# Coefficient-network loads and first-projection stores moved from SyncE to GpSimd in a four-layer vision kernel

## The chip, the cores and the metric

The kernel runs on one core of one Trainium2 chip. The metric is the device time of one execution in microseconds (us). Before the change it is 5452.3 us, the median of three runs (5446.23 to 5452.5). The kernel works in float32 throughout.

The engines are named as the profile names them: PE (TensorE), DVE (VectorE), ACT (ScalarE), POOL (GpSimd) and SP (SyncE). SP computes nothing here: it only begins DMAs. POOL and ACT can begin DMAs as well, each in the order of its own instruction stream.

## The reference

A batch of 8 images of 56 x 56 positions and 192 channels passes four residual layers, each `x = x + layer(groupnorm(x))`. Layers 0 and 1 are Toeplitz layers, layer 2 is a 7 x 7 depthwise convolution with an MLP, layer 3 is window attention. The change concerns layers 0 and 1, which compute:

```python
p = silu(x @ p_w.T + p_b); q = silu(x @ q_w.T + q_b); v = silu(x @ v_w.T + v_b)   # 192 -> 576
a1 = rpe_mlp(positions, t1_...) * decay     # positions -55..55; 4 small layers 1->32->32->32->32->576
a2 = rpe_mlp(positions, t2_...) * decay     # decay = (0.95 + 0.05*clip(slope, 0, 1)) ** |distance|
qv = q * v
o1 = toeplitz(qv along w, a1); o2 = toeplitz(qv along h, a2)
out = (p * (o1 + o2)) @ o_w.T + o_b
```

So each of the two layers needs two tables of coefficients (111 distances by 576 channels), and each table comes out of a small network of width 32 (the coefficient network) and a decay per channel. The tables don't depend on x.

## The kernel before

**Work on x.** Images go in pairs of pairs: `j0` is 0 or 2, and stands for four images. `tno_qv` (L224) is the first projection: it loads x in groups of 256 positions (L240, tile name `t6`, three buffers), normalizes on ACT (L246), multiplies with the q and v weights on PE (L263, or L284 for the first two groups), adds the bias on DVE (L272, tile `t8`, three buffers), applies silu on ACT (L301), multiplies q by v on POOL (L304, tile `t4`, three buffers) and stores the product in DRAM (L307). The stores are held back by one unit: `multiply` begins with the store of the unit before. One unit is 128 positions by up to 512 of the 1152 columns; a full unit's store is 128 partitions of eight rows of 512 bytes, 512 KB.

`tno_toeplitz` (L365) reads that product back (L380, L383), reads 32 x 60 blocks of the table (L393), and multiplies on PE (L406). ACT copies the result out (L413), DVE turns it (L424, L426), POOL adds the second direction (L429) and stores the sum (L436). `tno_out` (L484) does the rest of the layer.

**Tables.** `decay_tables` (L136) is a generator that makes the two tables of one layer. It loads the slopes 128 channels at a time into a tile of two buffers (L145), raises them to powers on DVE (L146 to L158), then for each of two networks loads its small arrays with six DMAs (L165 to L174, two buffers of each, shared by both layers), runs the three hidden layers (PE L180, DVE L182), and for each 128 channels the last layer (PE L187), clears a tile's end on POOL (L191), multiplies with the decay on DVE (L194) and stores the result in DRAM as a table (L204: four DMAs of 512 rows of 240 bytes per 128 channels).

**Order.** `tno_layers` (L681) writes the order of the first part out by hand. First come the statistics of x (L210, L217), then the first projection of layer 0 for `j0` = 0 in two generators: `first` (columns 0 to 511, all positions) and `rest` (columns 512 to 1151). The loop at L730 takes, for each of 28 turns, a piece of the statistics of the other images, a unit of `first` or `rest`, and a step of each layer's `decay_tables`. On PE, DVE, ACT and POOL the instructions stand in exactly this order. SP's stream is made from the same program: a DMA of SP stands where the program begins it, so a DMA that must wait holds up all that stand behind it. In the built program each DMA of SP also waits until the DMA eight places before it on SP has landed, as they share eight semaphores in turn; the DMAs of POOL have eight of their own.

After that come five lanes, made by `weave` (L644). A lane is a list of generators run one after the other with the pieces of one `tno_toeplitz` woven in at a rate given by estimated times. The Toeplitz generator's first piece only begins its first loads and is counted at 8.0 (L451); the computing pieces count 3.2 each. The pieces are given out when the lane's work has passed the share `lo` (0.04 if not set) and are all out at `hi` (0.92). Lane 0 holds what is left of `rest` and then the projection of the other four images; lanes 1 to 3 hold the rest of layers 0 and 1. The SBUF of the table stage (pool `tab`) is given up before lane 0, and the Toeplitz tiles (pool `tz`) take its place, so in the built program the first loads of lane 0 wait for the last table stores of both layers.

Of the kernel before, what the change touches and what calls it, by code (L numbers as in the profile page):

```python
# [12 lines left out]
F32 = mybir.dt.float32  # L13
# [18 lines left out]
D1 = 576  # L32
# [11 lines left out]
class Net:  # L44
# [91 lines left out]
    def decay_tables(self, L, p, tables):  # L136

        nc, inp = self.nc, self.inp
        tv = p.tile([32, 111], F32, name=f"{L}tv", bufs=1)
        nc.sync.dma_start(tv, inp["tvec"])  # L140
        pows = []
        for c in range(5):
            m = min(128, D1 - 128 * c)
            sl = p.tile([128, 1], F32, name=f"{L}sl")
            nc.sync.dma_start(sl[:m], inp[f"{L}_slope"][128 * c : 128 * c + m, :])  # L145
            nc.vector.tensor_scalar(sl[:m], sl[:m], 0.0, 1.0, ALU.max, ALU.min)  # L146
            nc.vector.tensor_scalar(sl[:m], sl[:m], 1.0 - 0.95, 0.95, ALU.mult, ALU.add)
            pw = p.tile([128, 64], F32, name=f"{L}pw", bufs=5)
            nc.gpsimd.memset(pw[:m, 0:1], 1.0)
            n = 1  # L150
            while n < 64:
                nc.vector.tensor_scalar(
                    pw[:m, n : 2 * n], pw[:m, 0:n], sl[:m], None, ALU.mult
                )
                n *= 2
                if n < 64:
                    sq = p.tile([128, 1], F32, name=f"{L}sl")
                    nc.vector.tensor_mul(sq[:m], sl[:m], sl[:m])  # L158
                    sl = sq
            pows.append(pw)  # L160
            yield 1.0
        for d in range(2):
            t = f"{L}_t{d + 1}"
            w0 = p.tile([32, 2], F32, name="w0")
            nc.sync.dma_start(w0[:, 0:1], inp[f"{t}_w0"])  # L165
            nc.sync.dma_start(w0[:, 1:2], inp[f"{t}_b0"])
            ws = p.tile([32, 3, 32], F32, name="ws")
            nc.sync.dma_start(ws, inp[f"{t}_ws"])
            bs = p.tile([32, 3], F32, name="bs")
            nc.sync.dma_start(bs, inp[f"{t}_bs"])  # L170
            wo = p.tile([32, D1], F32, name="wo")
            nc.sync.dma_start(wo, inp[f"{t}_wo"])
            bo = p.tile([128, 5], F32, name="bo")
            nc.sync.dma_start(bo, inp[f"{t}_bo"])  # L174
            h = p.tile([32, 111], F32, name=f"{L}h")
            nc.vector.tensor_scalar(h, tv, w0[:, 0:1], w0[:, 1:2], ALU.mult, ALU.add)
            nc.vector.tensor_scalar(h, h, 0.0, None, ALU.max)
            for i in range(3):
                hp = self.bank2()[:32, 0, :111]
                nc.tensor.matmul(hp, ws[:, i, :], h, start=True, stop=True)  # L180
                h = p.tile([32, 111], F32, name=f"{L}h")
                nc.vector.tensor_scalar(h, hp, bs[:, i : i + 1], 0.0, ALU.add, ALU.max)  # L182
                yield 1.0
            for c in range(5):
                m = min(128, D1 - 128 * c)
                ap = self.bank2()[:, 0, :111]
                nc.tensor.matmul(  # L187
                    ap[:m], wo[:, 128 * c : 128 * c + m], h, start=True, stop=True
                )
# [31 lines left out]
        for more in self.all_norms():  # L221
            pass

    def tno_qv(self, L, j0, xs, gn, qv, apart=None, cols=(0, 2 * D1), g0=0):  # L224

        nc, p, inp = self.nc, self.tp, self.inp
# [68 lines left out]
        def multiply(m, n, z, at, c0):  # L297
            k = n // 128
            for f in stores:
                f()  # L300
            nc.scalar.activation(z[:m, :n, :], z[:m, :n, :], AF.Silu)  # L301
            prod = p.tile([128, 4, DC * 4], F32, name="t4")
            half = z[:m, :n, :].rearrange("p (n h c) b -> p n h (c b)", h=2, c=DC)
            nc.gpsimd.tensor_mul(prod[:m, :k], half[:, :, 0], half[:, :, 1])  # L304
            n0 = c0 // 128
            stores[:] = [
                lambda: nc.sync.dma_start(  # L307
                    qv[2 * n0 : 2 * n0 + 2 * k, at : at + m, :].rearrange("n t e -> t n e"),
                    prod[:m, :k].rearrange("p n (h e) -> p (n h) e", h=2),
                )  # L310
            ]
# [53 lines left out]
    def tno_toeplitz(self, j0, mats, qv, o):  # L365
# [82 lines left out]
        for n in range(2):  # L448
            loaded.append(load(n))
            matrices(n)  # L450
        yield 8.0  # L451

        work = []

# [226 lines left out]
    def tno_layers(self, x0, x1, x2, gn, last):  # L681
# [18 lines left out]
        with ExitStack() as ctx, ExitStack() as wqp:  # L700
# [2 lines left out]
            Q = lambda i, j0, *more: self.tno_qv(LS[i], j0, x[i], gn[i], qvs[j0], *more)  # L703
            O = lambda i, j0, woven=True: self.tno_out(LS[i], j0, x[i], gn[i], o[i], x[i + 1], gn[i + 1], woven)
            TZ = lambda i, j0: self.tno_toeplitz(j0, tables[i], qvs[j0], o[i])
            QT, OT, TZT = 25 * 2.25 * 5.3, 28 * 10.7, 8 + 72 * 3.2

            with tc.tile_pool(name="tab", bufs=2) as tab:
                stats = [self.input_stats(x0, gn[0], j, tab) for j in range(4)]
                for more in stats[0]:  # L710
                    pass
                first, rest = Q(0, 0, tab, (0, 512)), Q(0, 0, None, (512, 2 * D1), 2)
                next(first)

# [12 lines left out]
                decay = [self.decay_tables(LS[i], tab, tables[i]) for i in range(2)]  # L727
                more = (dt for st in stats[2:] for dt in st)
                with tc.manual_schedule(engines=ENGINES):
                    for n in range(28):  # L730
                        next(more, None)
                        if n == 18:
                            next(rest)
                        if next(first, None) is None:
                            next(rest)
                        if n < 21:
                            next(decay[0])
                        if n >= 7:
                            next(decay[1])
                        if n in (14, 21):  # L740
                            qv = qvs[0 if n == 14 else 2]
                            to = qv[:, T:].rearrange("n (p k) e -> p n (k e)", p=112)
                            nc.gpsimd.dma_start(to, view(none, 0, [[0, D1 // 32], [1, 512]]))
                    for more in decay:
                        assert next(more, None) is None
                lanes = [[(rest, QT * 5 / 9 * 21 / 25 - 25.0), (Q(0, 2), QT)], [(O(0, 0), OT), (Q(1, 0), QT)]]
                parts = [Q(1, 2, None, cols) for cols in ((0, 512), (512, 2 * D1))]
                lanes += [[(O(0, 2), OT), (parts[0], QT * 4 / 9)], [(parts[1], QT * 5 / 9), (O(1, 0), OT)]]
                lanes += [[(O(1, 2, False), OT)]]
            in_order = tc.manual_schedule(engines=ENGINES)  # L750
            with tc.tile_pool(name="tz", bufs=1) as self.tz, in_order:
# [1 line left out]
                for i in range(2):  # L753
                    self.tms.append(self.tz.tile([128, 32 * self.TW], F32, name=f"tm{i}"))
                for n, tz in enumerate((TZ(0, 0), TZ(0, 2), TZ(1, 0), TZ(1, 2))):
                    self.weave(lanes[n], tz, lanes[n + 1][0][0], TZT)
                wqp.close()
            self.weave(lanes[4], **last())

# [915 lines left out]
```

## Time and profile before

| | |
|---|---|
| median of three runs | 5452.3 us |
| the profiled execution's own time | 5448.52 us |
| its span, first to last instruction | 5446.5 us |
| busy: PE, DVE, ACT, POOL | 5166.3, 2588.6, 2384.0, 1767.5 us |
| mean granted PE clock | 0.978 |
| DMA moved | 1116.48 MB, 205 GB/s on average |
| first matmul of the projection | at 27.82 us |
| first Toeplitz matmul | at 378.06 us |

A profile page gives busy times by engine, the span in 40 slices, DMA queues (q1 is the hardware queue of SP, q10 that of ACT, q0 the software queue of POOL), groups of instructions by line, and DMA issues. "Idle before, releaser" says what ended the idle time of an engine ahead of an instruction. A waits view sums those by the instruction that waited: total us, times, longest. A windows view gives the busy time of each engine in a stretch. Lines are L numbers of the kernel before.

### The profile page before, as it was taken

Reading aid. Unit: us, or ns where it says so; the run is one execution under the profiler, and the core shown is the slowest. Engines: PE = TensorE matmul, PEld = TensorE weight load, DVE = VectorE, ACT = ScalarE, POOL = GpSimd, SP = SyncE. Lnnn points to the kernel's source line nnn. Section 1 sums busy time; section 2 is a strip of 40 time slices with the busy share of each in tenths; the row PEclk is TensorE's granted clock in tenths of the full one; section 3 lists DMA queues with packets and bytes.
Section 4 is the critical chain, followed back from the end, with each engine's and each line's share of the span. In section 5 each row is a group of like instructions: output and inputs, shape, how many; then the busy total and the mean of one; then the engine's idle time right before and its main releaser. Section 6 shows DMA issues by size and latency. Waiting matters only on the chain.

```text
span 5446.5 us, 144346 instructions
## 1 busy us (share of the span) xinstructions
PE 5166.3 (95%) x64672; PEld 3811.3 (70%) x64672; DVE 2588.6 (48%) x3990; ACT 2384.0 (44%) x3179; POOL 1767.5 (32%) x1291
## 2 busy tenths in 40 slices
PE   7879999999999999999999899989999999999998
PEld 4657777777777777777777778855665444777776
DVE  6535556455555555645566322422212331566665
ACT  3345555444554454655454322242323333444443
POOL 2225675233664333645443100000001100333333
PEclk9889999999999999999999999999999999999999
DMA  7699997887786999888897666634444221445442
GB/s 253 149 242 280 289 315 228 274 279 256 248 267 170 327 309 308 277 233 280 296 325 246 205 219 237 221 127 161 140 165 121 74 69 49 84 97 108 99 103 68
DMA packets 1051146, 1116.48 MB, mean 205 GB/s; under 512 B 235200, under 2 KB 986304, under 8 KB 1036128
## 3 DMA queue, kind: packets, MB, share of 16 engines
q1 hardware_dynamic: 911584, 854.88, 52.7%
q0 software_dynamic: 38144, 200.99, 9.6%
q10 hardware_dynamic: 100800, 51.38, 3.7%
q8 instruction: 508, 8.32, 0.6%
q14 instruction: 110, 0.90, 0.1%
HBM read 743.17 MB, written 363.94 MB: 203 GB/s over the span
## 4 chain that ended last, share of the span: by engine, by line
PE 49%; DMA 3%; DVE 2%; issue 1%; ACT 1%; POOL 1%; SPq 1%; ACTq 0%; POOLq 0%; DVEq 0%
PE bank L976 7%; PE bank L837 5%; PE bank L1056 5%; PE bank L1250 4%; PE bank L263 3%; PE bank L592 3%; PE bank L1070 3%; PE bank L536 3%; PE bank L1366 2%; PE bank L1280 2%; PE bank L1197 2%; PE bank L1321 2%; PE bank L586 1%; PE bank L406 1%; PE bank L1340 1%
## 5 line engine op out<-in xcount | busy, mean ns | idle before, releaser
L263 PE MATMUL bank<-wq,t 128*128 128x256 f32 (+4 forms) x7680 | 1289.1, 374 | 73.5 <-DVE t L272 43.7
L263 PEld LDWEIGHTS bank<-wq,t 128*128 128x128 f32 (+2 forms) x7680 | 1004.9, 190 | 351.6 <-issue 92.5
L272 DVE TENSOR_TENSOR t<-bank,wq 128x1024 f32<-128x1024 f32 (+3 forms) x480 | 517.7, 1112 | 691.4 <-PE bank L263 540.9
L304 POOL TENSOR_TENSOR t<-t 128x1024 f32<-128x1024 f32 (+2 forms) x288 | 528.4, 1848 | 673.9 <-ACT t L301 338.5
L413 ACT COPY ot<-bank 128x896 f32<-128x896 f32 x576 | 493.2, 909 | 511.5 <-PE bank L406 401.8
L429 POOL TENSOR_TENSOR s<-s,ot 128x1568 f32<-128x1568 f32 x128 | 550.9, 4305 | 197.4 <-DVE ot L426 137.7
L301 ACT ACTIVATE t<-t 128x2048 f32<-128x2048 f32 (+2 forms) x288 | 423.2, 1488 | 330.5 <-DVE t L272 320.5
L406 PE MATMUL bank<-q,tm 56*32 56x224 f32 x18432 | 505.1, 354 | 18.7 <-DMA tm<-L_tab 11.6
L406 PEld LDWEIGHTS bank<-q,tm 56*32 56x32 f32 x18432 | 340.2, 106 | 145.3 <-issue 84.1
L122 POOL DMA_DIRECT2D x<-t x112 | 87.0, 777 | 1087.6 <-DVE t L601 1022.9
L555 ACT ACTIVATE bank<-bank,wo 128x448 f32<-128x448 f32 x448 | 262.9, 606 | 386.2 <-PE bank L545 361.2
L560 DVE TENSOR_TENSOR t<-t,bank 128x896 f32<-128x896 f32 x224 | 242.7, 1087 | 397.8 <-ACT bank L555 339.8
L976 PE MATMUL bank<-z,w 128*128 128x448 f32 (+1 forms) x1344 | 414.4, 556 | 1.5 <-ACT h L985 1.5
L536 PE MATMUL bank<-t,wo 128*128 128x224 f32 x1792 | 372.0, 361 | 21.4 <-ACT t L515 10.2
L536 PEld LDWEIGHTS bank<-t,wo 128*128 128x128 f32 x1792 | 334.9, 192 | 51.0 <-issue 30.2
L592 PE MATMUL bank<-t,wo 128*128 128x224 f32 x1792 | 368.9, 359 | 0.0
L592 PEld LDWEIGHTS bank<-t,wo 128*128 128x128 f32 x1792 | 329.9, 190 | 31.2 <-issue 31.2
L837 PEld LDWEIGHTS bank<-xt,cm 113*112 113x112 f32 x3072 | 316.1, 180 | 42.8 <-issue 33.9
L837 PE MATMUL bank<-xt,cm 113*112 113x108 f32 (+2 forms) x3072 | 324.4, 265 | 10.8 <-ACT h L985 5.7
L976 PEld LDWEIGHTS bank<-z,w 128*128 128x128 f32 (+1 forms) x1344 | 183.0, 189 | 206.7 <-issue 198.7
L127 POOL DMA_DIRECT2D x<-x x64 | 36.7, 574 | 843.4 <-DVE x L1007 813.5
L424 DVE STREAM_TRANSPOSE s<-ot 128x1792 f32<-128x1792 f32 x144 | 292.8, 2034 | 23.0 <-ACT ot L413 14.8
(162 smaller groups left out, 6972.8 us busy)
## 6 DMA issues: line engine op xcount, KB each, us to landing
q<-qv SPq DMA_DIRECT2D x36, 3584.0 KB
t<-L_sum SPq DMA_DIRECT2D x112, 1008.0 KB
L_sum<-s POOLq DMA_DIRECT2D x256, 392.0 KB, 7.3
qv<-t SPq DMA_DIRECT2D x192, 512.0 KB
cm<-in_L_cm SPq DMA_DIRECT2D x96, 896.0 KB
tm<-L_tab SPq DMA_DIRECT2D x288, 240.0 KB
q<-qv SPq DMA_DIRECT2D x40, 1568.0 KB
q<-qv ACTq DMA_DIRECT2D x32, 1568.0 KB
```

Source lines behind the costliest of these rows:

```text
L263: nc.tensor.matmul(pp[:m, b, 256 * j : 256 * j + k], x[rows, j, 2 if part else b, s : s + m], w[rows, part, c0 + c : c0 + c + k],  start=p ...
L272: nc.vector.tensor_add(z[:m, c : c + k, :], view(pp[:m], 0, [[1, k], [256, 4]]), view(bias[:m], c0 + c, [[1, k], [0, 4]]),)
L301: nc.scalar.activation(z[:m, :n, :], z[:m, :n, :], AF.Silu)
L304: nc.gpsimd.tensor_mul(prod[:m, :k], half[:, :, 0], half[:, :, 1])
L406: nc.tensor.matmul(pt[32 * j : 32 * j + 32, r, hf * 224 : (hf + 1) * 224], tm[rows, at : at + 32], q[rows, :, 4 * c : 4 * c + 4], start=Tr ...
L413: nc.scalar.copy(view(ot, 4 * (g % 4), [[16, 2], [32, 112], [1, 4]]), view(pt, 0, [[512, 2], [4, 112], [1, 4]]),)
L424: nc.vector.transpose(to, of.rearrange("p (i k) -> p i k", k=32))
L429: add.tensor_add(to, to, view(of, 0, [[1, 28], [32, 56]]))
L536: mm(gs[c // 2][:, b, c % 2 * 256 : c % 2 * 256 + N], pw[:, 0, 128 * c : 128 * c + 128], xn[:, b], start=c % 2 == 0, stop=False,)
L592: mm(P[:, b, :N], ow[:, c, 0:128], g[:, 4 * b + c], start=False, stop=c == 3)
L837: nc.tensor.matmul(pc[:, 128 * e + 4 * m0 : 128 * e + 4 * m1], cm[:113, e, k, :], xt[:, m0 - 1 + k : m1 - 1 + k, c + e, :], start=n == 0 a ...
L976: nc.tensor.matmul(phs[c][:, s, :TT], w0[rows, part, at : at + 128], z[rows, Z[2 if part else s], :], start=part == flip, stop=part != flip,)
```

## The change

The 36 small loads of the two layers' coefficient networks, slopes and positions become 32 DMAs of POOL that stand ahead of all projection work. The slopes of a layer come in two DMAs into one tile. The arrays of the four networks (two layers, two networks) share tiles of 128 partitions, each network on its own 32, so that none waits for another to give up a buffer; `h` and the PSUM results of the hidden layers lie on the same partitions. `tvec` is loaded once per network.

The stores of the first projection of layer 0, `j0` = 0 (`first` and `rest`, 75 DMAs) are begun by POOL in place of SP; all other projections keep SP. The first piece of every Toeplitz generator is counted at 18.0 in place of 8.0, and lane 0 begins its loads at 0.02 of its work in place of 0.04.

In the built program PE, DVE, ACT and POOL carry the same arithmetic in the same order up to lane 0; SP loses 111 DMAs and POOL gains 107. In lane 0 the first Toeplitz matmuls stand behind 24 more matmuls of the projection than before, in lanes 1, 2 and 3 behind 80, 56 and 64 more of the lane's own (counted as the program counts them).

```diff
     def decay_tables(self, L, p, tables):
-        tv = p.tile([32, 111], F32, name=f"{L}tv", bufs=1)
-        nc.sync.dma_start(tv, inp["tvec"])
+        slopes = p.tile([128, 5], F32, name=f"{L}slopes", bufs=1)
+        of = inp[f"{L}_slope"]
+        nc.gpsimd.dma_start(slopes[:, 0:4], of[:512, 0].rearrange("(c p) -> p c", p=128))
+        nc.gpsimd.dma_start(slopes[:64, 4:5], of[512:D1, :])
+        nets = []
+        for d in range(2):
+            t = f"{L}_t{d + 1}"
+            at = slice(64 * (L == "L1") + 32 * d, 64 * (L == "L1") + 32 * d + 32)
+            if at.start == 0:
+                one = lambda n, shape: p.tile([128, *shape], F32, name=f"net{n}", bufs=1)
+                self.nets = one("t", [111]), one("w0", [2]), one("ws", [3, 32]), one("bs", [3]), one("wo", [D1])
+            bo = p.tile([128, 5], F32, name=f"{t}bo", bufs=1)
+            tv, w0, ws, bs, wo = net = [n[at] for n in self.nets]
+            nc.gpsimd.dma_start(w0[:, 0:1], inp[f"{t}_w0"])
+            nc.gpsimd.dma_start(w0[:, 1:2], inp[f"{t}_b0"])
+            nc.gpsimd.dma_start(tv, inp["tvec"])
+            for to, n in ((ws, "ws"), (bs, "bs"), (wo, "wo"), (bo, "bo")):
+                nc.gpsimd.dma_start(to, inp[f"{t}_{n}"])
+            nets.append((at, *net, bo))
+        yield 0.0
...
-            sl = p.tile([128, 1], F32, name=f"{L}sl")
-            nc.sync.dma_start(sl[:m], inp[f"{L}_slope"][128 * c : 128 * c + m, :])
+            sl = slopes[:, c : c + 1]
...
-            w0 = p.tile([32, 2], F32, name="w0")
-            nc.sync.dma_start(w0[:, 0:1], inp[f"{t}_w0"])
...
-            bo = p.tile([128, 5], F32, name="bo")
-            nc.sync.dma_start(bo, inp[f"{t}_bo"])
-            h = p.tile([32, 111], F32, name=f"{L}h")
+            at, tv, w0, ws, bs, wo, bo = nets[d]
+            h = p.tile([128, 111], F32, name=f"{L}h")[at]
...
             stores[:] = [
-                lambda: nc.sync.dma_start(
+                lambda: (by or nc.sync).dma_start(
...
         for n in range(2):
             loaded.append(load(n))
             matrices(n)
-        yield 8.0
+        yield 18.0
...
-            QT, OT, TZT = 25 * 2.25 * 5.3, 28 * 10.7, 8 + 72 * 3.2
+            QT, OT, TZT = 25 * 2.25 * 5.3, 28 * 10.7, 18 + 72 * 3.2
...
-                first, rest = Q(0, 0, tab, (0, 512)), Q(0, 0, None, (512, 2 * D1), 2)
+                first, rest = (
+                    Q(0, 0, *more, nc.gpsimd) for more in ((tab, (0, 512), 0), (None, (512, 2 * D1), 2))
+                )
+                decay = [self.decay_tables(LS[i], tab, tables[i]) for i in range(2)]
+                for more in decay:
+                    next(more)
                 next(first)
...
-                decay = [self.decay_tables(LS[i], tab, tables[i]) for i in range(2)]
...
-                    self.weave(lanes[n], tz, lanes[n + 1][0][0], TZT)
+                    self.weave(lanes[n], tz, lanes[n + 1][0][0], TZT, lo=0.04 if n else 0.02)
```

More of the change, by code (lines that the diff above doesn't have):

```diff
@@ L162, in decay_tables @@
         for d in range(2):
-            t = f"{L}_t{d + 1}"
-            w0 = p.tile([32, 2], F32, name="w0")
-            nc.sync.dma_start(w0[:, 0:1], inp[f"{t}_w0"])
[L166 to L172, printed above, removed]
-            bo = p.tile([128, 5], F32, name="bo")
-            nc.sync.dma_start(bo, inp[f"{t}_bo"])
-            h = p.tile([32, 111], F32, name=f"{L}h")
+            at, tv, w0, ws, bs, wo, bo = nets[d]
+            h = p.tile([128, 111], F32, name=f"{L}h")[at]
             nc.vector.tensor_scalar(h, tv, w0[:, 0:1], w0[:, 1:2], ALU.mult, ALU.add)
@@ L178, in decay_tables @@
             for i in range(3):
-                hp = self.bank2()[:32, 0, :111]
+                hp = self.bank2()[at, 0, :111]
                 nc.tensor.matmul(hp, ws[:, i, :], h, start=True, stop=True)
-                h = p.tile([32, 111], F32, name=f"{L}h")
+                h = p.tile([128, 111], F32, name=f"{L}h")[at]
                 nc.vector.tensor_scalar(h, hp, bs[:, i : i + 1], 0.0, ALU.add, ALU.max)
@@ L222, in input_stats, with tno_qv @@
             pass
-    def tno_qv(self, L, j0, xs, gn, qv, apart=None, cols=(0, 2 * D1), g0=0):
+    def tno_qv(self, L, j0, xs, gn, qv, apart=None, cols=(0, 2 * D1), g0=0, by=None):
         nc, p, inp = self.nc, self.tp, self.inp
```

## The prediction

> **What bounds the kernel now.** The shares of the page come first: PE is busy for 5166.3 of 5446.5 us, so at most 280 us are to be had by feeding it better. Where they lie I read from the windows view (columns: length; busy us of PE, PEld, DVE, ACT, POOL with instructions; granted clock; DMA share; GB/s):
>
> ```profile
> 28.00:92.00 64.00, 62.91 (x212) 27.28 (x212) 34.26 (x55) 24.82 (x29) 16.35 (x10) 0.95 0.71 232
> 92.00:245.00 153.00, 119.25 (x606) 92.32 (x605) 94.80 (x248) 61.41 (x72) 42.40 (x35) 0.84 0.56 160
> 245.00:378.00 133.00, 101.85 (x602) 79.09 (x600) 45.31 (x69) 49.54 (x64) 37.62 (x35) 0.86 1.01 227
> 378.00:480.00 102.00, 97.61 (x1359) 74.99 (x1360) 51.38 (x40) 62.40 (x78) 53.30 (x33) 0.98 0.93 273
> 480.00:800.00 320.00, 304.99 (x4168) 234.37 (x4167) 179.00 (x132) 175.22 (x199) 210.21 (x120) 0.98 0.93 296
> ```
>
> From 92 to 378 us, the stage that makes the tables beside the projection, PE stands still for 65 us (153 - 119.3 and 133 - 101.9) at a clock of 0.84 to 0.86. From 378 to 800 only 19 us are idle. The first half has a DMA share of 0.56, the second of 1.01: the second is also at the limit of the DMA engines. Who ends PE's waits from 92 to 380, by the waits view (total us, times, longest):
>
> ```profile
> PE bank L180 <- issue: 19.5, 3, 9.3
> PE bank L406 <- DMA tm<-L_tab: 11.6, 1, 11.6
> PE bank L180 <- DVE L1h L177: 9.9, 1, 9.9
> PE bank L263 <- DVE t L272: 8.6, 4, 5.5
> PE bank L263 <- ACT t L246: 6.3, 1, 6.3
> PE bank L187 <- DMA wo<-in_L_t_wo: 3.9, 1, 3.9
> ```
>
> L180 and L187 are the coefficient networks. Two of these waits name a DMA; behind those that name DVE the order of time on DVE shows more (start, us, idle before):
>
> ```profile
> 182.03 0.15 DVE L146 TENSOR_SCALAR L1sl<-L1sl 128x1 f32<-128x1 f32 x1 [5.23 <-DMA L1sl<-in_L_slope]
> 190.34 2.32 DVE L158 TENSOR_TENSOR L1sl<-L1sl 128x1 f32<-128x1 f32 x1
> 202.80 0.14 DVE L146 TENSOR_SCALAR L1sl<-L1sl 64x1 f32<-64x1 f32 x1 [5.66 <-DMA L1sl<-in_L_slope]
> ```
>
> DVE works without a gap from 157 to 207 but for two waits for slopes, and a third of 2.00 at 113.82: 12.9 us. The slope load stands on SP behind a store that waits for POOL:
>
> ```profile
> SPq L307 <- POOL t L304: 87.7, 28, 15.4
> POOL t L304 <- DMA qv<-t: 86.2, 17, 30.4
> ```
>
> The first line is SP's (0 to 450 us): SP waited 87.7 us for products it was to store, with loads and table stores behind. The second is POOL's (60 to 480): it waited for buffers whose stores hadn't landed, once for 30.4 us, when SP was held at the first Toeplitz loads.
>
> **What the Trainium skill says.** "DMA: Bandwidth & Descriptors", section "Issuing engines are not separate DMA queues": DMAs of all engines share the same 16 DMA engines, so another issuer saves sequencer time, not bandwidth. The trace agrees where it can: the share is 1.01 while SP and POOL both had DMAs out (245 to 378). Same page, section "SWDGE vs HWDGE vs iDMA": GpSimd's descriptors are made in software, in packets of preferably up to 4096 B, and each DMA engine turns between the two kinds of queue at packet borders. The trace agrees on size: a zero fill of POOL (L743) of 2 KB rows made 1024 packets of 4.03 KB. The queues' rows give the rates, bytes over share times span:
>
> ```profile
> q1 hardware_dynamic: 911584, 854.88, 52.7%
> q0 software_dynamic: 38144, 200.99, 9.6%
> ```
>
> q1 moves 298 GB/s of full share, q0 384. "SBUF — State Buffer", section "Who interferes with whom": a DVE instruction with two SBUF inputs and a GpSimd instruction that reads SBUF exclude each other. The trace agrees: the L158 above takes 2.32 us in place of 0.15 while L304 runs (190.27 to 192.64).
>
> **The change part by part**, against the profiled span.
>
> *Loads at the start.* POOL begins 32 DMAs. The nearest rows of its groups:
>
> ```profile
> L436 POOL DMA_DIRECT2D L_sum<-s x256 | 137.3, 539 | 21.0 <-POOL s L429 18.7 <-issue 2.2
> L122 POOL DMA_DIRECT2D x<-t x112 | 87.0, 777 | 1087.6 <-DVE t L601 1022.9 <-DVE st L604 53.2 <-DVE t L523 7.9
> L743 POOL DMA_DIRECT2D qv<-none x2 | 2.3, 1170 | 0.0
> ```
>
> 32 x 0.54 to 0.78 are 17 to 25 us, hidden as POOL's first product comes at 70.81; without that cover they would be on the path. At eight in flight and 5.1 us to landing (L726's row) they need at least 20. The fills of L726 behind them move from 2 to about 25 us and are needed after 350. On the DMA engines, at 1.05 share here, they add rows: 2432 against 896 that SP sent before 58 us. The nearest price is a table row of 240 B: from 254 to 262 us 5061 packets took 118.6% of 16 x 8 us, 30 ns each; from 167 to 180, 20 ns. So 1536 / 16 x 20 to 30 ns is 1.9 to 2.9 us more, and about half of all (2432 / 32 x 30 ns = 2.3) falls ahead of the first projection matmul, where DVE follows the landing of x. I take **+2**, bounds 0 and +6.
>
> *Slopes without waits.* The 12.9 us on DVE go. In the two long cases POOL had finished L304 by then; now DVE's operations meet it and one stretches by 2.2 us, as at 190.34. 12.9 - 2 x 2.2 is 8.5. From 97 to 135 DVE stays the bound (L272, powers and L218 make 6.1 us per unit against PE's 5.65), so the 8.05 us gap of PE ahead of 134.33 keeps most. **-8**, bounds -13 and -5.
>
> *Stage 245 to 378.* Four waits of PE: 9.31 ahead of L180 at 282.97 (DVE behind POOL's L191, behind table stores): half, -5; 3.90 for `wo`: all; 6.35 for x, whose load stood on SP behind a 7.64 us store: -5; 11.65 for tm: -9, since lane 0's loads stand on SP right behind the last table stores where five stores and an x load stood (339 to 352), and PE has 24 more matmuls, 7.3 us, to do first. After each wait 32 matmuls take 7.49 to 7.72 us in place of 5.65: -5 in all. Sum -28. The DMA engines allow less: their 134 us of work lose 6 us (17 stores, 7.5 MB: 25.5 us at 294 GB/s, measured on SP's stores and x from 80 to 90, against 19.5 at q0's 384) and 10 us of second q load that the first Toeplitz matmul doesn't need. 245 - 6 + 118 is 357; PE alone gives 378 - 6 - 28 + 7 = 351, with 7.3 us of work brought forward. The middle of both: **-23**, bounds -28 and -8.
>
> *Stores on POOL.* 75 of 1024 rows (or 256), unseen: between 384 rows (0.78) and 2016 (1.17), 0.9 us. The floor is 0.54; the ceiling is 2.7, as POOL took its next instruction 5.4 us after beginning the 2016-row fill at 234.38. I take 0.9, since L304 starts within 0.02 us of L436's end. POOL is busy for 96 of 318 us up to 378: hidden by idle POOL. From 378 to 480 31 stores add 28 to 53.3 of 102 us: still hidden, and its 30.4 us wait goes: **-2**, bounds -8 and +34. Behind a waiting POOL DMA stand L304, L191 and L429, and behind L304 DVE's L272 through `t8`.
>
> *Later first Toeplitz piece.* In lanes 1 to 3 the Toeplitz work starts 20 us later. PE is at 88% there (87.94 of 100 from 900 to 1000) against 99.8 once woven: up to 2 us a lane, made good in part: **+2**, bounds 0 and +6.
>
> Sum: +2 - 8 - 23 - 2 + 2 = -29, a span of 5417.5. Execution was 2.0 us over the span, and the median of runs 3.8 us over that, so I set it against the median: 5452.3 - 29 = 5423.3, rounded to **5423**.
>
> **The rivals.** *DMA engines bound, half the gain:* the share of 1.01 from 245 on and 0.93 up to 800 leaves no room; x and q loads are late by what POOL's packets take. For it: the two windows. Against: PE was fed at 0.93. -14: **5438**. If the last table stores, which lane 0's loads await in both programs, land no sooner, 9 us of the -23 stay too; that is within this case. *Given back:* lane 0 to its end at about 970 is paced by DMA, and an earlier start only waits later; only the start of lane 1 shifts: -3, **5449**. Against: the Toeplitz products take 95 to 97% of PE there. *Slower, POOL becomes the bound:* 102 - 53.3 us take 31 stores of 1.6 us; each 1 us more costs 31, so at 2.5 us the gain is gone and at 2.9 the kernel is 0.2% slower; at 3.0 **5466**. For it: software descriptors, 1024 rows each. Against: the 1.17 us row and the 2.7 us ceiling.
>
> **How the numbers follow.** Chances: forecast 0.64 (its own range 5404 to 5437, from the sums of the smaller and larger bounds without the tail of the store price), DMA bound 0.18, given back 0.10, slower 0.08. About 0.2%, 11 us, is what a measurement of this kernel can tell from no change. DMA bound splits 0.14 faster and 0.04 within, given back 0.02 and 0.08: faster 0.80, same 0.12, slower 0.08. The range leaves out the slower case at the top and the forecast's best tenth at the bottom: 5398 to 5450.
>
> **What would show it.** No DVE wait at the slopes; PE idle from 92 to the first L406 down from 65 to about 35 us; first L406 near 356 with no long tm wait; POOL's stores at 0.9 us; SP without waits for L304 until lane 0's second projection; q0 bytes up by 29 MB. Wrong if x arrives over 6 us later, if stores take over 2 us of POOL, or if the gaps reappear after 378.

## The result, and the profile after

The changed kernel takes 5474.6 us (median), the kernel before 5448.5 us on the same chip: a ratio of 1.0038, 95% interval 1.0027 to 1.0049. It is slower by about 21 us (15 to 27), where 5423 us and a gain had been forecast. The ratio is not that of the two medians (1.0048): one of the 15 executions, at 6530.8 us and a granted clock of 0.746, is left out, and the means of the rest are 5470.2 and 5449.6 us. From here on 0.001 of a ratio is read as 5.5 us, and every ratio is against the kernel before on the same chip, as its median was 5449 to 5462 us from one occasion to another.

The same windows of the kernel after (columns as before: length; busy us of PE, PEld, DVE, ACT, POOL with instructions; granted clock; DMA share; GB/s):

```profile
28.00:92.00 64.00, 60.16 (x201) 26.24 (x201) 33.76 (x56) 24.07 (x30) 17.09 (x16) 0.95 0.68 234
92.00:245.00 153.00, 119.58 (x587) 90.62 (x586) 103.90 (x244) 59.87 (x68) 63.84 (x57) 0.85 0.53 153
245.00:378.00 133.00, 106.05 (x635) 82.08 (x635) 49.66 (x73) 54.19 (x71) 61.19 (x60) 0.88 0.91 217
378.00:480.00 102.00, 85.52 (x1112) 65.47 (x1110) 43.81 (x35) 49.13 (x63) 55.03 (x41) 0.92 0.77 263
480.00:800.00 320.00, 303.00 (x4152) 232.10 (x4151) 177.25 (x131) 175.96 (x202) 212.54 (x129) 0.98 0.89 290
```

PE's idle time from 92 to 378 is 60.4 us (153 - 119.58 and 133 - 106.05), where it was 65 and should have become 35 or so. And a new hole stands behind it: from 378 to 480 PE is busy for 85.5 us in place of 97.6. The DMA share went down, to 0.91 and 0.77, so no more was moved in these windows than before; which transfer came late is another question (below). The waits view of PE from 92 to 480 us (total us, times, longest) says what ends the waits now:

```profile
PE bank L186 <- issue: 25.1, 4, 11.3
PE bank L269 <- ACT t L252: 21.1, 3, 14.7
PE bank L269 <- ACT ot L419: 12.2, 2, 10.2
PE bank L269 <- DVE t L278: 8.8, 7, 2.3
PE bank L412 <- DMA tm<-L_tab: 3.6, 1, 3.6
```

The wait for `wo` is gone and the long wait for `tm` has shrunk from 11.65 to 3.57 us, as forecast, but the matmul behind it comes later than before (389.31 in place of 378.06), so the shorter wait is no gain. The waits ahead of the coefficient networks (L186, L180 before) are 25.1 us in place of 29.4. In place of the others PE waits for ACT's normalization (L252, L246 before), which waits for x. The waits of POOL (60 to 480 us) did shrink as forecast; the line answers the 86.2 us of before:

```profile
POOL t L310 <- DMA qv<-t: 8.6, 3, 4.2
```

The queues' rows show the 29 MB that moved to POOL:

```profile
q1 hardware_dynamic: 850992, 825.59, 50.3%
q0 software_dynamic: 47424, 230.32, 11.4%
```

How far the profiled execution lags behind the one before, read from the starts of the same work in both PE timelines:

| work | before | after | lag |
|---|---|---|---|
| first projection matmul | 27.82 | 31.71 | 3.9 |
| first bias addition of the loop (DVE, L272 / L278) | 97.34 | 102.31 | 5.0 |
| second bias addition | 103.42 | 115.00 | 11.6 |
| first matmul of layer 1's first coefficient network | 209.87 | 215.69 | 5.8 |
| first Toeplitz matmul | 378.06 | 389.31 | 11.3 |
| first matmul of `tno_out` (L536 / L542) | 948.3 | 973.3 | 25.0 |
| end of the span | 5446.5 | 5475.1 | 28.6 |

Three losses stand out: the start, the stretch between the first and the second bias addition, and lane 0. After lane 0 little is added.

### The profile page after: what moved, and what is told of

The parts are those of the page before. It is cut to its first block, busy times and chain, and to the rows that moved or that the text cites. A ratio compares the mean times of both kernels' runs of the same rounds, so it can differ in the third digit from the quotient of the medians.

```text
span 5475.1 us, 144317 instructions
## 1 busy us (share of the span) xinstructions
PE 5188.1 (95%) x64672; PEld 3825.2 (70%) x64672; DVE 2597.3 (47%) x3990; ACT 2382.4 (44%) x3179; POOL 1848.3 (34%) x1398
## 3 DMA queue, kind: packets, MB, share of 16 engines
q0 software_dynamic: 47424, 230.32, 11.4%
## 4 chain that ended last, share of the span: by engine, by line
PE 77%; DMA 6%; DVE 6%; issue 3%; POOL 3%; ACT 3%; SPq 2%; ACTq 0%; DVEq 0%; POOLq 0%
PE bank L269 16%; PE bank L986 7%; PE bank L598 6%; PE bank L542 6%; PE bank L412 5%; PE bank L847 5%; PE bank L1066 5%; PE bank L1260 4%; PE bank L592 3%; PE bank L1080 3%; PE bank L551 2%; PE bank L1376 2%; PE bank L1290 2%; DMA qv<-t 2%; PE bank L1207 2%
## 5 line engine op out<-in xcount | busy, mean ns | idle before, releaser
L278 DVE TENSOR_TENSOR t<-bank,wq 128x1024 f32<-128x1024 f32 (+3 forms) x480 | 517.6, 1112 | 713.6 <-PE bank L269 591.5
L419 ACT COPY ot<-bank 128x896 f32<-128x896 f32 x576 | 493.2, 909 | 506.9 <-PE bank L412 388.5
L542 PE MATMUL bank<-t,wo 128*128 128x224 f32 x1792 | 372.8, 361 | 16.2 <-DVE t L566 5.9
L542 PEld LDWEIGHTS bank<-t,wo 128*128 128x128 f32 x1792 | 335.4, 192 | 46.0 <-issue 26.4
L598 PEld LDWEIGHTS bank<-t,wo 128*128 128x128 f32 x1792 | 330.0, 190 | 31.4 <-issue 31.4
```

Source lines behind the costliest of these rows:

```text
L278: nc.vector.tensor_add(z[:m, c : c + k, :], view(pp[:m], 0, [[1, k], [256, 4]]), view(bias[:m], c0 + c, [[1, k], [0, 4]]),)
L419: nc.scalar.copy(view(ot, 4 * (g % 4), [[16, 2], [32, 112], [1, 4]]), view(pt, 0, [[512, 2], [4, 112], [1, 4]]),)
L542: mm(gs[c // 2][:, b, c % 2 * 256 : c % 2 * 256 + N], pw[:, 0, 128 * c : 128 * c + 128], xn[:, b], start=c % 2 == 0, stop=False,)
L598: mm(P[:, b, :N], ow[:, c, 0:128], g[:, 4 * b + c], start=False, stop=c == 3)
```

## The experiments

The expectations of the first four runs, in us, were written against a before of 5448, where the chip used gave 5462; they are compared as differences. One theory was that the order on SP had changed (A), the rival that POOL's packets slow x down wherever they run (B).

### The three parts of the change, one by one

Loads and stores without the weave's numbers:

```diff
-        yield 18.0
+        yield 8.0
-            QT, OT, TZT = 25 * 2.25 * 5.3, 28 * 10.7, 18 + 72 * 3.2
+            QT, OT, TZT = 25 * 2.25 * 5.3, 28 * 10.7, 8 + 72 * 3.2
-                    self.weave(lanes[n], tz, lanes[n + 1][0][0], TZT, lo=0.04 if n else 0.02)
+                    self.weave(lanes[n], tz, lanes[n + 1][0][0], TZT)
```

> Only the weave's numbers are put back (first Toeplitz piece 8.0, lo 0.04 everywhere); loads and stores stay with GpSimd. Theory A (order on SP): lo 0.02 puts the ten first Toeplitz loads ahead of one more x load of lane 0, which is why ACT waits 21 us for x and PE 10.2 us at 407.65. Then this kernel loses that gap: x load five stands ahead of the Toeplitz loads, time about 5462 (12 below the changed kernel), still above the kernel before by the 4 to 5 us of the late start and the x waits at 128 and 325. Theory B (GpSimd's packets): x lands late wherever GpSimd stores at the same time, whatever the order; then the time stays at 5471 to 5478 and a wait of 10 us for x near 400 stays.

The stores alone (kernel before, with the `by` of the change and `nc.gpsimd` for `first` and `rest`):

```diff
-                first, rest = Q(0, 0, tab, (0, 512)), Q(0, 0, None, (512, 2 * D1), 2)
+                first, rest = (
+                    Q(0, 0, *more, nc.gpsimd) for more in ((tab, (0, 512), 0), (None, (512, 2 * D1), 2))
+                )
```

> Only the stores of the first projection go to GpSimd; small loads and weave as before. Theory A: nothing is reordered around the Toeplitz loads and the start is as before (first projection matmul at 27.8), slopes come without waits as SP is free; the x loads that stand behind loads of the statistics or behind table stores may be late by 5 to 15 us in sum: 5440 to 5455. Theory B: the x waits at 325 and 400 stay in full, 5463 or more.

The small loads alone (the changed `decay_tables`, started ahead of `next(first)`, stores and weave as before):

```diff
+                decay = [self.decay_tables(LS[i], tab, tables[i]) for i in range(2)]
+                for more in decay:
+                    next(more)
                 next(first)
```

> Only the small loads go to GpSimd at the start; stores and weave as before. Both theories: first projection matmul about 4 us later (31.7 in place of 27.8), no waits for slopes on DVE and none for wo on PE. If the start passes to the end undiminished and the slopes give nothing on PE: 5452 to 5454; if the slopes give the 8 us forecast, 5444 to 5446.

The weave's numbers alone (the first diff the other way, in the kernel before):

> Only the weave's numbers are changed (18.0 and lo 0.02 for lane 0). Theory A: one x load of lane 0 goes behind the first Toeplitz loads on SP, a wait of PE for x of about 10 us after the first Toeplitz matmul: 5456 to 5460. Theory B: no change, 5446 to 5451.

| kernel | ratio | interval | us | first Toeplitz matmul |
|---|---|---|---|---|
| loads and stores | 1.0010 | 1.0004 to 1.0017 | +5.5 | 383.76 |
| stores | 1.0033 | 1.0021 to 1.0045 | +18 | 390.22 |
| loads | 0.9991 | 0.9984 to 0.9998 | -5 | 375.67 |
| weave | 1.0022 | 1.0012 to 1.0031 | +12 | 398.7 |
| all (the change) | 1.0038 | 1.0027 to 1.0049 | +21 | 389.31 |

The loads gain, the stores and the weave lose. Taking the weave's numbers out of the change wins 15 us (12 had been expected), as theory A says; for the weave alone A's time came true, but not the wait it named (below). For the stores neither theory held: the loss is larger than A said, but the x wait of B at 325 isn't there (PE waits 1.37 and 0.29 us for x, at 324.00 and 325.48). Stores and loads together lose 7.5 us less than their sum: in the stores kernel PE still waits for `wo`, 5.82 us, and DVE for slopes, 12.2 us, which the early loads take away.

**The weave.** With `lo` 0.02 the first Toeplitz loads are begun one x load earlier in lane 0. SP's timeline of the changed kernel (start, length, what, and the number of DMAs):

```profile
353.09 0.66 SPq L246 DMA_DIRECT2D t<-in_x  x1
356.19 9.56 SPq L386 DMA_DIRECT2D q<-qv  x2
365.80 14.62 SPq L399 DMA_DIRECT2D tm<-L_tab  x4
380.47 0.61 SPq L389 DMA_DIRECT2D q<-qv  x1
381.12 6.20 SPq L399 DMA_DIRECT2D tm<-L_tab  x4
387.46 12.04 SPq L246 DMA_DIRECT2D t<-in_x  x3
```

Since 299 us four x loads stand ahead of the Toeplitz loads here; before there were five, the fifth at 347.10, ahead of the Toeplitz loads that began at 351.79. In before's timeline:

```profile
347.10 1.07 SPq L240 DMA_DIRECT2D t<-in_x  x1
351.19 0.36 SPq L307 DMA_DIRECT2D qv<-t  x1
351.79 8.49 SPq L380 DMA_DIRECT2D q<-qv  x2
```

The fifth now stands behind eleven DMAs and is begun at 387.46. ACT and PE, in their timelines, show what follows (in brackets the idle time ahead and what ended it):

```profile
403.76 3.06 ACT L252 ACTIVATE t<-t,gn 128x256 f32<-128x256 f32 x6 [21.19 <-DMA t<-in_x]
```

```profile
407.65 7.98 PE L269 MATMUL bank<-wq,t 128*128 128x256 f32 x32 [10.20 <-ACT ot L419]
```

PE's record names `ot` of L419, which is ACT's next work; the cause is one line up, ACT standing behind x. In the kernel with the weave's numbers alone, where SP begins the stores too, another chain carries the loss. The fifth x load is passed over there as well (begun at 376.08), but ACT isn't seen to wait for it. The stores of the projection stand behind the same eleven DMAs, and POOL, DVE and PE wait for them in turn:

```profile
387.37 3.02 POOL L304 TENSOR_TENSOR t<-t 128x1024 f32<-128x1024 f32 x2 [32.63 <-DMA qv<-t]
389.74 3.04 DVE L272 TENSOR_TENSOR t<-bank,wq 128x512 f32<-128x512 f32 x3 [26.01 <-POOL t L304]
390.49 8.28 PE L263 MATMUL bank<-wq,t 128*128 128x256 f32 x32 [19.32 <-DVE t L272]
```

POOL's wait isn't new: it was 30.41 us before. But before, PE had Toeplitz matmuls to do from 378.06 on, while here more of the projection stands ahead of the first of them, and that projection waits.

**The stores.** The loss begins at 98 us. DVE's timeline of the stores kernel:

```profile
98.03 2.36 DVE L272 TENSOR_TENSOR t<-bank,wq 128x1024 f32<-128x1024 f32 x2 [4.21 <-PE bank L263]
...
105.06 0.21 DVE L152 TENSOR_SCALAR L0pw<-L0pw,L0sl 128x1 f32<-128x1 f32 x1 [4.42 <-POOL L0pw L149]
105.19 0.15 DVE L158 TENSOR_TENSOR L0sl<-L0sl 128x1 f32<-128x1 f32 x1
105.37 3.10 DVE L152 TENSOR_SCALAR L0pw<-L0pw,L0sl 128x2 f32<-128x2 f32 x1
...
111.39 2.34 DVE L272 TENSOR_TENSOR t<-bank,wq 128x1024 f32<-128x1024 f32 x2
```

and POOL's:

```profile
99.68 0.93 POOL L307 DMA_DIRECT2D qv<-t  x1 [0.30 <-POOL t L304]
100.63 2.38 POOL L304 TENSOR_TENSOR t<-z 128x1024 f32<-128x1024 f32 x1
103.30 0.93 POOL L307 DMA_DIRECT2D qv<-t  x1 [0.30 <-POOL t L304]
104.25 0.74 POOL L304 TENSOR_TENSOR t<-z 128x256 f32<-128x256 f32 x1
104.92 0.11 POOL L149 MEMSET L0pw<- 128x1 f32 x1
105.28 0.75 POOL L307 DMA_DIRECT2D qv<-t  x1 [0.26 <-POOL L0pw L149]
106.05 2.36 POOL L304 TENSOR_TENSOR t<-t 128x1024 f32<-128x1024 f32 x1
```

In the kernel before, the clear and the same L152 were:

```profile
97.84 0.10 POOL L149 MEMSET L0pw<- 128x1 f32 x1
100.37 0.23 DVE L152 TENSOR_SCALAR L0pw<-L0pw,L0sl 128x2 f32<-128x2 f32 x1
```

A store takes POOL 0.93 us (0.65 to 0.98 over the 75 of the changed kernel) and, where it stands right behind a product of POOL's own, 0.30 us ahead of it. From 70 to 106 us POOL has little room for that: it was busy for 24.1 of those 36 us and is busy for 32.0 now. So the clear of the first power (L149), a store or two behind in POOL's stream, comes at 104.92 in place of 97.84. DVE waits for it, and then loses again where its power steps meet POOL's late work: L152 takes 3.10 us where it took 0.23. The Trainium skill, "SBUF — State Buffer", section "Who interferes with whom", counts `tensor_scalar` among the operations that can, where their operands allow it, enter a two-port mode and then exclude GpSimd from the shared port pair, and be excluded by it; the trace agrees in that the 3.10 us end with POOL's L304 (108.41). They began ahead of that product, while POOL was beginning a store (105.28 to 106.03). The second bias addition is at 111.39 in place of 103.42, and PE stands still for 2.6 us at 112.65, behind DVE, and for 4.5 us at 124.46, behind ACT, whose silu and normalization follow DVE.

### Where the stores lose

The first twelve stores (the products of 71 to 106 us) back on SP, the other 63 on POOL:

```diff
-                lambda: (by or nc.sync).dma_start(
+                lambda: (by if by and not (apart and at < 2 * GT) else nc.sync).dma_start(
```

> The stores alone on GpSimd, but the first twelve (products of the first two groups of 256 positions) stay on SP; small loads and weave as before. Theory C (GpSimd's stream is full from 71 to 105 us): with the twelve stores gone from it, the first L149 clears at about 98 and not at 104.9, DVE doesn't wait 4.4 us for it, the statistics' buffers come free on time, and PE's two waits of 2.6 and 4.5 us at 112 and 124 are gone: 8 of the 18 us that the stores alone cost, 5470 to 5472 where before is 5462. Theory D (the loss of the stores sits after 245 us, in the transfers): still 5478 to 5481.

All 75 on POOL, the clear by DVE:

```diff
-            nc.gpsimd.memset(pw[:m, 0:1], 1.0)
+            nc.vector.memset(pw[:m, 0:1], 1.0)
```

> The stores alone on GpSimd, all 75, with one more difference: the first power's L149 clear is done by DVE in place of GpSimd. If it is this clear, queued behind the stores, that makes DVE late at 100 us, the 4.4 us wait of DVE goes and PE's 2.6 and 4.5 us at 112 and 124 mostly with it: 8 to 10 us of the 18. If it is the products L304, and so the buffers, that are late behind the stores, DVE's clear changes nothing: 17 to 19 above before.

With twelve stores back on SP the ratio is 1.0014 (1.0005 to 1.0023), 8 us over before: some 10 of the 18 us are gone. In PE's timeline the first matmul of layer 0's network, at 134.33 before and 142.86 in the stores kernel, is back:

```profile
135.15 0.54 PE L180 MATMUL bank<-L0h,ws 32*32 32x111 f32 x2 [6.50 <-issue]
```

The clear alone does less. The ratio is 1.0021 (1.0011 to 1.0030), 12 us over before, between the two expectations and with an interval that overlaps that of the stores kernel. In the trace the same matmul comes at 142.00. DVE no longer waits for POOL, but runs its power steps into POOL's late stores and products instead:

```profile
101.08 1.54 DVE L158 TENSOR_TENSOR L0sl<-L0sl 128x1 f32<-128x1 f32 x1
...
102.97 0.81 DVE L152 TENSOR_SCALAR L0pw<-L0pw,L0sl 128x4 f32<-128x4 f32 x1
...
105.04 3.01 DVE L152 TENSOR_SCALAR L0pw<-L0pw,L0sl 128x32 f32<-128x32 f32 x1
```

The 0.81 us at 102.97 fall within a store that POOL was beginning (102.89 to 103.82), with no product beside it:

```profile
102.89 0.93 POOL L307 DMA_DIRECT2D qv<-t  x1 [0.30 <-POOL t L304]
```

So the clear was the first wait to be seen, not the whole cause; the cause is the twelve stores in POOL's stream, which make its work of 98 us some 7 us late and bring it into DVE's power steps. How much of it is lateness and how much the stores' own meeting with DVE was not told apart.

What the other 63 stores cost, 8 us, isn't settled. With twelve stores on SP PE waits 9.65 us for `wo` where it waited 3.90 before. But the wait for x behind it, 6.35 us before, is gone, and the first matmul that x feeds comes 3.4 us late (317.05 in place of 313.69) where the network's matmul ahead of both waits was 4.3 us late already.

### The start

The small loads in their new tiles, but begun by SP behind the x loads of the second statistics (from 29.7 to 53.3 us):

```diff
-        nc.gpsimd.dma_start(slopes[:, 0:4], of[:512, 0].rearrange("(c p) -> p c", p=128))
+        nc.sync.dma_start(slopes[:, 0:4], of[:512, 0].rearrange("(c p) -> p c", p=128))
...
                 for more in stats[1]:
                     pass
+                decay = [self.decay_tables(LS[i], tab, tables[i]) for i in range(2)]
+                for more in decay:
+                    next(more)
```

> The small loads alone, in their own tiles and all at once, but begun by SP behind the x loads of the second statistics (about 30 to 45 us) and not by GpSimd at the start. If the late start of the loads kernel (first projection matmul at 30.96 in place of 27.82) comes from small rows on the DMA engines ahead of x, the matmul is back at 27.8 and the time is 3 us below the loads kernel: 8 us below before. If the start is late for another reason, or if what is saved by 100 us is lost at the transfers of 245 to 378 us, it stays at 5 below before.

The first projection matmul is at 27.81 us (30.96 with the loads on POOL, 27.82 before), so the late start came from the small rows that POOL begins ahead of x (their place and their queue changed together here). The ratio is 0.9988 (0.9977 to 0.9999), lower than 0.9991 as expected, but the intervals overlap; the 3 us are shown by the trace and not by the times.

### What bounds 245 to 378 us

In the kernel with the loads alone the forecast gain is there early and then melts. PE's timeline:

```profile
203.38 0.55 PE L186 MATMUL bank<-L1h,netws 32*32 32x111 f32 x2 [4.61 <-issue]
...
278.50 0.55 PE L186 MATMUL bank<-L1h,netws 32*32 32x111 f32 x2 [10.34 <-issue]
...
309.94 8.47 PE L269 MATMUL bank<-wq,t 128*128 128x256 f32 x32 [11.86 <-ACT t L252]
...
375.67 3.24 PE L412 MATMUL bank<-q,tm 56*32 56x224 f32 x64 [12.26 <-DMA tm<-L_tab]
```

The first line is 6.5 us ahead of before (209.87) in spite of a start 3.1 us late, the last 2.4 us ahead. Between them PE waits longer for x and for `tm`. In the kernel before:

```profile
282.97 0.54 PE L180 MATMUL bank<-L1h,ws 32*32 32x111 f32 x2 [9.31 <-issue]
...
313.69 7.72 PE L263 MATMUL bank<-wq,t 128*128 128x256 f32 x32 [6.35 <-ACT t L246]
```

The wait of 3.90 us for `wo` stood between these two. It is gone with the early loads, but nothing comes of it: from the network's matmul to the one that x feeds are 31.4 us now (278.50 to 309.94) and were 30.7. PE only gets to the wait for x sooner. The kernel with the weave's numbers alone, which up to lane 0 is the kernel before, had the same by chance in its profiled execution: no wait for `wo`, 12.80 us for x, 31.3 us in all. So the two waits count once, and x sets them. With the stores on POOL as well this stretch is shorter, 25.2 us in the loads-and-stores kernel, but it begins 11.4 us later than before (294.33).

In this stage the DMA share is 0.99, and GpSimd's second zero fill of 4 MB (L743) is under way: begun at 288.2 us it took 18.4 us to land before, and 27.2 us, begun at 292.6, in the changed kernel. So both fills were moved, in the kernel before, to a stage with room (from 150 to 240 us the DMA share was 0.33 to 0.57; they are begun at 158 and 209 us now):

```diff
-                        if n in (14, 21):
-                            qv = qvs[0 if n == 14 else 2]
+                        if n in (7, 12):
+                            qv = qvs[0 if n == 7 else 2]
```

> The kernel before with one difference: the two zero fills of 4 MB that GpSimd begins at turns 14 and 21 (234 and 288 us) are begun at turns 7 and 12 (about 155 and 215 us). Theory E (from 245 to 378 us the DMA engines are the limit, so taking waits off the queues there can't pay): some 20 us of DMA work leave the stage, x no longer waits 6.35 us at 313, the tables and first Toeplitz loads land earlier, first Toeplitz matmul at 360 to 370 in place of 378, 8 to 15 us faster. Rival (the stage is set by the order of waits on SP and DVE, as the prediction had it): at most the 6 us of the x wait, 0 to 6 us faster.

The ratio is 0.9980 (0.9973 to 0.9987), 11 us faster than before by moving two DMAs. The windows view and PE's timeline of this kernel:

```profile
245.00:378.00 133.00, 112.64 (x786) 87.12 (x785) 48.01 (x75) 59.52 (x75) 38.68 (x36) 0.91 0.96 206
```

```profile
285.46 0.54 PE L180 MATMUL bank<-L1h,ws 32*32 32x111 f32 x2 [4.88 <-issue]
...
304.10 5.65 PE L263 MATMUL bank<-wq,t 128*128 128x256 f32 x32
...
370.23 3.24 PE L406 MATMUL bank<-q,tm 56*32 56x224 f32 x64 [15.47 <-DMA tm<-L_tab]
```

The wait for x is gone with no change to what SP begins, and from the network's matmul to the one that x feeds are 18.6 us in place of 30.7; the gap of 9.31 is halved. In return PE is 7.9 us late at 217.81 (209.87 before): beside the first fill DVE waits 7.72 us for slopes, and a wait of PE for DVE grows from 5.51 us at 187 to 7.95 at 183. The gain is beyond the 0 to 6 us of the rival. So theory E stands: what the prediction read as order was in good part a full set of DMA engines. The two fills were moved together, and what each was worth isn't known. The gap ahead of 282.97 ended before the second fill was begun and after the first had landed (253.3 us), in a stretch with a DMA share of 1.15 (253 to 288 us; 1.06 with the fills moved). The wait for `tm` isn't shortened.

### The weave's two numbers apart

The changed kernel with `lo` 0.04 everywhere, 18.0 kept:

```diff
-                    self.weave(lanes[n], tz, lanes[n + 1][0][0], TZT, lo=0.04 if n else 0.02)
+                    self.weave(lanes[n], tz, lanes[n + 1][0][0], TZT)
```

> The changed kernel with lo 0.04 for lane 0 again; 18.0, small loads and stores as changed. If the share lo 0.02 is what puts an x load behind the first Toeplitz loads, the 10 us wait at 407.65 is gone and the time is that of the kernel with loads and stores alone or a few us better, as 18.0 lets PE do more of the lane while tm lands: 2 to 6 us above before. If 18.0 is what costs (the Toeplitz pieces of all lanes come later), it stays 15 to 20 us above before.

The ratio is 1.0012 (1.0004 to 1.0019), that of loads and stores without either number (1.0010), and just above the 2 to 6 us expected. PE's wait of 10.20 us at 407.65 is one of 1.65 us at 402.70. So the 14 us between this and 1.0038 are those of `lo`, and 18.0 costs and gains nothing that can be seen beside these loads and stores.

### All corrections together, and a version that beats both

The changed kernel with the three corrections (loads on SP as above, twelve stores on SP, `lo` 0.04):

> The changed kernel with three corrections, one for each cause found: small loads begun by SP behind the x loads of the second statistics, the first twelve stores back on SP, lo 0.04 in lane 0 (18.0 and the other 63 stores on GpSimd stay). If these three make up the whole loss, the sum of what they gave one by one (3 for the start, 10 for the twelve stores, 14 for lo) is taken from the 20 us over before: 5 to 8 us below before. If something else in the stores costs (DMA packets of GpSimd, its place on the sequencer after 105 us), it stays within 3 us of before or above.

0.9990 (0.9982 to 0.9999), about 5 us below before: in line with the sum, so no large fourth cause is left. But the loads on SP give as much alone (0.9988): the stores that stay on POOL gain nothing.

The loads on SP and the early fills, with the stores and the weave of before:

> The small loads on SP behind the x loads of the second statistics, and the zero fills at turns 7 and 12; stores and weave as before. The gains of 245 to 378 us then no longer run into the DMA engines: x doesn't wait at 311, first Toeplitz matmul at 360 to 367. If the two add up, 18 to 21 us below before; if both only reach the same limit at the first Toeplitz loads, 12 to 14 below.

0.9955 (0.9941 to 0.9970), 5438.2 us where before took 5460.5: 24 us faster (16 to 32), at least the sum of its parts (7 and 11). The first Toeplitz matmul is at 353.73, earlier than the 360 to 367 expected. A possible reason, not tested apart: DVE has no wait for slopes here, where it waited 7.72 us beside the first fill in the kernel with the fills alone.

In addition the first two Toeplitz units of each lane begin their table loads ahead of their q loads:

```diff
         for n in range(2):
-            loaded.append(load(n))
             matrices(n)
+            loaded.append(load(n))
```

> The kernel with loads on SP and earlier fills, with one more difference: the first two Toeplitz units of each lane begin their table loads (L399) ahead of their q loads and not behind them. If PE's wait for tm at the first Toeplitz matmul (11.9 us there) is the place of tm behind 3.1 MB of q on SP, tm and q land together at about 340 to 347 where the matmul began at 353.7, and the time falls by up to 8 us: 23 to 31 below before. If the bytes and the DMA engines set it, q is late in place of tm, the matmul stays at 352 to 356, and the time stays at 20 to 25 below before.

0.9954 (0.9941 to 0.9968), 5422.9 us where before took 5449.1: no different. PE's timeline shows why:

```profile
345.02 0.92 PE L412 MATMUL bank<-q,tm 56*32 56x224 f32 x2 [4.79 <-DMA q<-qv]
355.12 3.24 PE L412 MATMUL bank<-q,tm 56*32 56x224 f32 x62 [9.18 <-DMA q<-qv]
```

PE now waits for q in place of `tm`, and goes on at 355.12 (353.73 without this edit). The DMA share from 320 to 355 us is 1.01 (1.06 without the edit). The bytes set this wait, not their order.

## Why the prediction was wrong

Taken by its own steps:

**Loads at the start, +2 (0 to +6).** Right in mechanism and inside the bounds: the first projection matmul is 3.1 to 3.9 us later. That these rows delay it is shown by the kernel that sends them later and from SP.

**Slopes without waits, -8 (-13 to -5).** Right for the loads alone: 6.5 us ahead at 203.38 with a start 3.1 us late is 9.6. In the changed kernel the stores took it back, as DVE was late from 98 us on and stretched by POOL's products.

**Stores on POOL, -2 (-8 to +34): this step failed first.** The price of beginning a store was right, 0.93 us against 0.9, though the 0.30 us that POOL waits right behind a product were not in it. The cover was wrong. "96 of 318 us up to 378: hidden by idle POOL" is an average over stages; from 70 to 106 us POOL was busy for two thirds of the time, and with the stores in it its stream held DVE up. And the list of what stands behind a POOL DMA (L304, L191, L429) left out L149, the clear in the middle of the slopes' chain. That clear was only a part: done by DVE, it gave back some 6 of the 18 us, within the noise, and DVE ran into POOL's late work instead. The twelve stores there cost some 10 us, all 75 alone 18. That is inside the bound of +34, but by another route than the rival that was written: its price of 2.5 us per store never came near.

**Stage 245 to 378, -23 (-28 to -8): failed as well.** The sum adds four waits of PE as if each were lost time of its own. The 3.90 us for `wo` went, but with the loads alone the wait for x behind it grew by 5.5; with loads and stores the two fell by 4.3, where 8.9 were counted, and in the changed kernel they grew by 4.5. The 9.31 us ahead of L180, of which half was to go, stayed at 9.4 to 12.3 in every other kernel that left the fills where they were. With loads and stores the first Toeplitz matmul is at 383.76 with a `tm` wait of 11.3 us, where -9 was counted on it. The two sums in the prediction (PE 351, DMA 357) were averaged, where of two such bounds the later one holds; and taken as the prediction takes them they leave 28 and 22 us, whose middle is 25 and not 23. But the larger error is that the stage is bound by transfers at each of its waits, and an earlier start of a transfer there takes its room from another. The rival "DMA engines bound, half the gain" saw this and was given 0.18; the fills show it was the better reading of the share of 1.01. The Trainium skill's sentence that the prediction used ("DMA: Bandwidth & Descriptors", section "Issuing engines are not separate DMA queues": another issuer saves sequencer time only) was cited and then not carried into this sum. The x wait's size isn't settled: 5.95 us in the loads-and-stores kernel and 14.74 in the changed one, though SP's order is the same up to there.

**The Toeplitz loads moved ahead.** This is the largest failure. The prediction booked as gain that lane 0's loads stand behind the last table stores "where five stores and an x load stood". With the stores on POOL that x load is what lane 0's projection needs next; passed over, it arrives at 403 us and `lo` costs about 14 us. "Wrong if x arrives over 6 us later" was the right alarm, with no price put to it.

**Later first Toeplitz piece, +2.** No cost and no gain was seen.

**The range.** The upper end of the forecast's own range, 5437, doesn't follow from the bounds as shown: with the stores at -2 the larger ones add up to -3 (6 - 5 - 8 - 2 + 6), so 5449. The measured loss lies beyond that too.

## What to carry to other kernels

Before work is put on an engine because it is idle, look at the engine in the very stretch where the work falls, and list every instruction behind it there, the small clears too; an average over 300 us hid a full stretch of 36. When a transfer is moved ahead, ask who needs what it passes. Waits that follow one another to the same late transfer count once. And in a stage with a DMA share near 1, reordering queues only changes which transfer is late: move bytes out of the stage instead.

## What the runs showed of the hardware that was not expected

- Moving two fills of 4 MB from 234 and 288 us to 158 and 209 was worth 11 us, more than what the small loads' change was worth. Such a fill took POOL 1.15 to 1.19 us to begin and 17 to 27 us to land (19.7 and 21.5 where they were moved).
- A store that POOL begins right behind its own product cost not 0.93 but some 1.23 us of its stream, as POOL waits 0.30 us for that product's end first (40 of the 75 in the changed kernel had a wait of this kind).
- DVE's small operations were stretched up to tenfold and more beside POOL's work (L152: 0.23 to 3.10 us, beside a store of 0.75 us and a product of 2.36 us in a row; 0.81 us beside a store alone), so a late POOL delayed DVE twice, by what DVE waited for and by what it met.
